# Pair products of 32 features: four stores per batch tile with batch-major rows, in place of five stores with partition-major rows

## The chip, the core and the metric

One core of a Trainium2 chip runs the whole kernel. TensorE (PE) multiplies matrices, VectorE (DVE) works elementwise, ScalarE (ACT) copies, SyncE (SP) here only issues transfers; 16 DMA engines move data between HBM and the on-chip memory SBUF, which has 128 partitions. PSUM takes the results of TensorE. The metric is device microseconds of one execution. All input and output is fp32.

## The reference

There are B = 4096 batch rows of F = 32 feature vectors of D = 64 numbers. For each of the 496 pairs of features (i, j) with i < j, vector i is multiplied by a 64x64 matrix of that pair, and the result is multiplied elementwise by vector j:

```python
i_idx, j_idx = np.triu_indices(F, k=1)
vi = inputs[:, i_idx, :]
vj = inputs[:, j_idx, :]
vdotw = jnp.einsum('bpd,pde->bpe', vi, W)
inter = vdotw * vj
return inter.reshape(B, -1)
```

A batch row gives 496 x 64 = 31,744 numbers, 126,976 bytes. The output has 520 MB, the input x 33.6 MB, the weights some 8 MB.

## The kernel before

**Tiles.** The batch is cut into NT = 32 tiles of 128 rows, one row per partition. Features are taken two at a time: pair p of the code (0 to 15) stands for features 2p and 2p+1, which give (31-2p) and (30-2p) blocks of 64 output columns, 61-4p blocks together. So pair 0 has 61 blocks and pair 15 has one. All weights stay in SBUF (w_sb, loaded once at L117); x is read tile by tile (load_x, L82 to L85), the next one at the start of each tile, on ACT's queue.

**Work in a tile.** For each pair the kernel goes over chunks of 512 columns. TensorE multiplies the transposed x by the weights of the two features into PSUM (L147), and DVE multiplies that by x and writes the product into SBUF: in one instruction for both features (L157), or in two (L166) where the second feature's chunk is shorter and the one-instruction form would write 64 columns past the end of its store's piece. That is so in the last chunk of the last pair of a store, and where the second feature has nothing left. TensorE also transposes the next tile's x at pairs 5 and 6 (L104), and ACT copies the result out of PSUM (L105).

**Stores and the ring.** DVE writes into one buffer, `ring` (L110), of RING = 28,160 elements per partition (110 KB). STORES (L18) groups the pairs; for each group the code takes the next piece of the ring, going back to 0 when the piece doesn't fit in what is left (L129 to L131), lets DVE fill it, and then SP issues one store of 128 rows for it (L172). A piece that overlaps an older store's piece can be written only when that store has landed. With blocks of 64 columns as the unit, the ring has 440 and the five groups have 118, 102, 86, 99 and 91, in sum 496. Each store is split over all 16 DMA engines, eight rows to an engine; in the trace a row is one packet, and each engine closes its share with a packet of 4 bytes.

**Where rows go.** Before the launch the host orders x as [P, NT, F*D] with the tile index moved to the front: partition p has batch rows 32p to 32p+31, one per tile. The output tensor is [P, NT * 31,744]; at L172 partition p of tile t writes to column t * cols + o0 of its own row. So rows of one store lie 32 x 126,976 = 4,063,232 bytes apart. Flattened, that is the batch order of the reference. x of one tile is one contiguous MB.

Of the kernel before, what the change touches and what calls it, by code (L numbers as in the profile page):

```python
# [1 line left out]

# [6 lines left out]

F32 = mybir.dt.float32  # L10
ALU = mybir.AluOpType

P = 128
BANK = 512
BANKS = 8
CHUNK = BANK

STORES = [[0, 1], [2, 3], [4, 5], [6, 7, 8], [9, 10, 11, 12, 13, 14, 15]]  # L18
PREFETCH_AT = [5, 6]
RING = 28160  # L20


@with_exitstack
def pair_bilinear_kernel(
    ctx: ExitStack,
    tc: tile.TileContext,
    x: bass.AP,
    w: bass.AP,
    out: bass.AP,
    F: int,  # L30
    D: int,
):

    nc = tc.nc
    NT = x.shape[0]
    NPR = F // 2

    width = [(F - 1 - i) * D for i in range(F)]
    off = [sum(width[:i]) for i in range(F)]  # L60
    cols = sum(width)
    woff = [sum(width[0 : 2 * p : 2]) for p in range(NPR)]
    store_w = [sum(width[2 * p] + width[2 * p + 1] for p in g) for g in STORES]

    const = ctx.enter_context(tc.tile_pool(name="const", bufs=1))
    xtpool = ctx.enter_context(tc.tile_pool(name="xT", bufs=2))
    psum = ctx.enter_context(tc.tile_pool(name="ps", bufs=1, space=bass.MemoryType.PSUM))

    ident = const.tile([P, P], F32, tag="ident", name="ident")
    make_identity(nc, ident)  # L70

    def runs(tl, a, b, n):

        ap = tl[:, a : a + n]
        return bass.AP(ap.tensor, ap.offset, [list(ap.ap[0]), [b - a, 2], list(ap.ap[1])])


    xbuf = [const.tile([P, (F + 1) * D], F32, tag=f"x{b}", name=f"x{b}") for b in range(2)]
    for xb in xbuf:
        nc.gpsimd.memset(xb[:, F * D :], 0.0)  # L80

    def load_x(t):  # L82
        xt = xbuf[t % 2]
        nc.scalar.dma_start(out=xt[:, : F * D], in_=x[t])
        return xt  # L85

    pring = psum.tile([P, BANKS * BANK], F32, tag="pring", name="pring")
    bank = 0

    def take_banks(n):  # L90

        nonlocal bank
        if bank + n > BANKS:
            bank = 0
        got = pring[:, bank * BANK : (bank + n) * BANK]
        bank = (bank + n) % BANKS
        return got

    def transpose_x(xT, t, xt, g):

        n = 2 * BANK // P
        pt = take_banks(2)
        for c in range(n):
            nc.tensor.transpose(pt[:, ts(c, P)], xt[:, ts(n * g + c, P)], ident)  # L104
        nc.scalar.copy(xT[:, ts(g, 2 * BANK)], pt)  # L105

    def new_xT(t):
        return xtpool.tile([P, NPR * P], F32, tag="xT", name=f"xT_{t}")

    ring = const.tile([P, RING], F32, tag="ring", name="ring")  # L110
    at = 0
    xs = {0: load_x(0)}

    w_sb = []
    for p in range(NPR):
        wp = const.tile([P, width[2 * p]], F32, tag=f"w{p}", name=f"w{p}")
        nc.sync.dma_start(out=wp, in_=w[:, woff[p] : woff[p] + width[2 * p]])  # L117
        w_sb.append(wp)

    xTs = {0: new_xT(0)}  # L120
    for g in range(2):
        transpose_x(xTs[0], 0, xs[0], g)

    for t in range(NT):
        xt, xT = xs.pop(t), xTs.pop(t)
        if t + 1 < NT:
            xs[t + 1] = load_x(t + 1)
        for s, group in enumerate(STORES):
            if at + store_w[s] > RING:  # L129
                at = 0  # L130
            osb = ring[:, at : at + store_w[s]]  # L131
            at += store_w[s]
            o0 = off[2 * group[0]]
            for p in group:
                if t + 1 < NT and p in PREFETCH_AT:
                    if t + 1 not in xTs:
                        xTs[t + 1] = new_xT(t + 1)
                    transpose_x(xTs[t + 1], t + 1, xs[t + 1], PREFETCH_AT.index(p))
                for c0 in range(0, width[2 * p], CHUNK):
                    n = [max(0, min(CHUNK, width[2 * p + h] - c0)) for h in range(2)]  # L140
                    half = -(-n[0] // BANK) * BANK
                    pm = take_banks(2 * half // BANK)
                    for b0 in range(0, n[0], BANK):
                        b1 = min(b0 + BANK, n[0])
                        for h in range(2):
                            if b0 < n[h]:
                                nc.tensor.matmul(  # L147
                                    pm[:, h * half + b0 : h * half + b1],
                                    xT[h * D : (h + 1) * D, ts(p, P)],
                                    w_sb[p][h * D : (h + 1) * D, c0 + b0 : c0 + b1],  # L150
                                    start=True,
                                    stop=True,
                                )
                    o = [off[2 * p + h] - o0 + c0 for h in range(2)]
                    xj = [(2 * p + h + 1) * D + c0 for h in range(2)]
                    if n[1] > half - BANK and o[1] + n[0] <= store_w[s]:
                        nc.vector.tensor_tensor(  # L157
                            runs(osb, o[0], o[1], n[0]),
                            runs(pm, 0, half, n[0]),
                            runs(xt, xj[0], xj[1], n[0]),  # L160
                            ALU.mult,
                        )
                    else:
                        for h in range(2):
                            if n[h]:
                                nc.vector.tensor_tensor(  # L166
                                    osb[:, o[h] : o[h] + n[h]],
                                    pm[:, h * half : h * half + n[h]],
                                    xt[:, xj[h] : xj[h] + n[h]],
                                    ALU.mult,  # L170
                                )
            nc.sync.dma_start(out=out[:, t * cols + o0 : t * cols + o0 + store_w[s]], in_=osb)  # L172


# [36 lines left out]
```

## Time and profile before

| | us |
|---|---|
| median of 4 runs | 1339.51 (1339.38 to 1339.66) |
| profiled execution, its own time | 1339.53 |
| its span on the page | 1337.8 |
| first store issued | 24.47 |
| last DVE instruction starts | 1318.2 |
| a store of 30,208-byte rows (3776 KB), issue to landing, median of 32 | 21.9 |
| x of one tile (1024 KB), issue to landing, median of 32 | 14.2 |
| DVE, 128x1024 product in one instruction, mean of 768 | 1.217 |

HBM is read for 41.94 MB and written for 520.09 MB, 420 GB/s over the span. The page's line of slices gives the mean busy share of the DMA engines as 9 tenths or more in every slice but the last of 40. How to read it: the span is what the profiler saw from the first to the last instruction; the execution's time is 1.7 us longer. A wait is put down to the releaser that came last. A DMA engine's packets in the trace overlap by a few ns, so that a busy share can go a little over 1.

### The profile page before, as it was taken

What the parts mean: (1) busy time and instruction counts of PE and PEld (TensorE: products, weight loads), DVE (VectorE), ACT (ScalarE), POOL (GpSimd) and SP (SyncE); (2) the same over time, 40 slices, a digit from 0 to 9 for tenths busy, and PEclk for the clock granted to TensorE, in tenths of its full rate; (3) what the DMA queues carried; (4) which work ended last, traced back from release to release, by engine and by line L of the source; (5) the groups of instructions that cost most, each with busy time, mean ns of one, the idle gap of its engine ahead of it and who ended that gap; (6) DMA issues with size and microseconds to landing.
All of it is one profiled execution on the core that took longest, in us unless ns stands there. A gap on an engine that the chain in (4) does not pass through costs nothing.

```text
span 1337.8 us, 13157 instructions
## 1 busy us (share of the span) xinstructions
PE 1142.3 (85%) x5376; PEld 511.6 (38%) x5376; DVE 1199.0 (90%) x1376; ACT 66.1 (5%) x65; POOL 0.9 (0%) x8
## 2 busy tenths in 40 slices
PE   7899888888988888988889989899798898888982
PEld 3344333333333443334333444334344333343431
DVE  5999889998998989989889989899898998999993
ACT  1000000000000000000000000000000000000000
POOL 0000000000000000000000000000000000000000
PEclk9999999998999989999999999999999999999997
DMA  9999999999999999999999999999999999999996
GB/s 395 427 430 433 432 427 432 425 429 432 431 428 431 423 424 431 427 424 427 418 426 417 425 435 403 429 417 427 429 419 411 430 420 432 423 413 432 422 424 272
DMA packets 30012, 562.89 MB, mean 421 GB/s; under 512 B 3456, under 2 KB 3840, under 8 KB 5376
## 3 DMA queue, kind: packets, MB, share of 16 engines
q1 hardware_dynamic: 25344, 528.49, 92.7%
q10 hardware_dynamic: 4608, 33.56, 6.0%
q8 instruction: 42, 0.69, 0.2%
q14 instruction: 18, 0.15, 0.0%
HBM read 41.94 MB, written 520.09 MB: 420 GB/s over the span
## 4 chain that ended last, share of the span: by engine, by line
DMA 43%; DVE 37%; PE 16%; issue 2%; DVEq 0%
DMA out_dram<-ring 42%; DVE ring L157 33%; PE pring L147 13%; DVE ring L166 4%; PE pring L104 3%; DMA x<-in_x_dram 1%; DVEq L157 0%; DVEq L166 0%
## 5 line engine op out<-in xcount | busy, mean ns | idle before, releaser
L157 DVE TENSOR_TENSOR ring<-pring,x 128x1024 f32<-128x1024 f32 (+3 forms) x1056 | 1114.9, 1100 | 115.7 <-DMA out_dram<-ring 53.5
L147 PE MATMUL pring<-w,xT 64*128 64x512 f32 (+4 forms) x4864 | 1074.9, 559 | 165.6 <-DVE ring L157 161.5
L147 PEld LDWEIGHTS pring<-w,xT 64*128 64x128 f32 x4864 | 451.1, 189 | 756.6 <-DVE ring L157 600.8
L105 ACT COPY xT<-pring 128x1024 f32<-128x1024 f32 x64 | 64.8, 1012 | 1193.4 <-PE pring L104 1154.9
L166 DVE TENSOR_TENSOR ring<-pring,x 128x64 f32<-128x64 f32 (+3 forms) x320 | 114.1, 381 | 3.7 <-DVE ring L157 0.5
L104 PE MATMUL pring<-ident,x 128*128 128x128 f32 x512 | 76.1, 296 | 8.3 <-DMA x<-in_x_dram 8.3
L104 PEld LDWEIGHTS pring<-ident,x 128*128 128x128 f32 x512 | 60.6, 151 | 47.8 <-issue 34.3
L105 ACT ACT_TABLE_LOAD x1 | 1.3, 1283 | 1.7 <-PEq L203 1.7
masks.py:199 POOL TENSOR_SCALAR_AFFINE_SELECT ident<-ident 128x128 f32<-128x128 f32 x1 | 0.3, 295 | 0.0
L80 POOL MEMSET x<- 128x64 f32 x2 | 0.2, 153 | 0.0
masks.py:197 POOL MEMSET ident<- 128x128 f32 x1 | 0.2, 205 | 0.3 <-POOLq L203 0.3
L203 POOL MEMSET const-bfloat16-1.0<- 128x1 bf16 x1 | 0.1, 102 | 0.0
L203 POOL MEMSET const-uint8-127<- 128x1 uint8 x1 | 0.1, 102 | 0.0
L203 POOL MEMSET const-float32-0.0<- 128x1 f32 x1 | 0.1, 99 | 0.2 <-issue 0.2
L203 POOL MEMSET const-float32-1.0<- 128x1 f32 x1 | 0.1, 99 | 0.0
## 6 DMA issues: line engine op xcount, KB each, us to landing
out_dram<-ring SPq DMA_DIRECT2D x32, 3776.0 KB, 21.9
out_dram<-ring SPq DMA_DIRECT2D x32, 3264.0 KB, 21.6
out_dram<-ring SPq DMA_DIRECT2D x32, 3168.0 KB, 22.4
out_dram<-ring SPq DMA_DIRECT2D x32, 2912.0 KB, 21.4
out_dram<-ring SPq DMA_DIRECT2D x32, 2752.0 KB, 21.5
x<-in_x_dram ACTq DMA_DIRECT2D x32, 1024.0 KB, 14.2
w<-in_w_dram SPq DMA_DIRECT2D x1, 992.0 KB, 7.3
w<-in_w_dram SPq DMA_DIRECT2D x1, 928.0 KB, 11.6
```

The source lines that it names most:

```text
L80: nc.gpsimd.memset(xb[:, F * D :], 0.0)
L104: nc.tensor.transpose(pt[:, ts(c, P)], xt[:, ts(n * g + c, P)], ident)
L105: nc.scalar.copy(xT[:, ts(g, 2 * BANK)], pt)
L147: nc.tensor.matmul(pm[:, h * half + b0 : h * half + b1], xT[h * D : (h + 1) * D, ts(p, P)], w_sb[p][h * D : (h + 1) * D, c0 + b0 : c0 + b1 ...
L157: nc.vector.tensor_tensor(runs(osb, o[0], o[1], n[0]), runs(pm, 0, half, n[0]), runs(xt, xj[0], xj[1], n[0]), ALU.mult,)
L166: nc.vector.tensor_tensor(osb[:, o[h] : o[h] + n[h]], pm[:, h * half : h * half + n[h]], xt[:, xj[h] : xj[h] + n[h]], ALU.mult,)
L203: nc = bacc.Bacc("TRN2", target_bir_lowering=False, num_devices=1)
```

## The change

The pairs are grouped into four stores in place of five. The groups have 118, 102, 123 and 153 blocks, rows of 30,208, 26,112, 31,488 and 39,168 bytes. The ring keeps its size and its rule. Batch rows are dealt out in their plain order: tile t has rows 128t to 128t+127, partition p has row 128t+p, and the output tensor is [B, 31,744]. Rows of one store then lie 126,976 bytes apart, and x needs no reordering on the host; x of one tile is still one contiguous MB. Which pair ends a group decides where L166 stands in for L157; no other instruction is touched.

```diff
-STORES = [[0, 1], [2, 3], [4, 5], [6, 7, 8], [9, 10, 11, 12, 13, 14, 15]]
+STORES = [[0, 1], [2, 3], [4, 5, 6], [7, 8, 9, 10, 11, 12, 13, 14, 15]]
...
-    NT = x.shape[0]
+    B = x.shape[0]
+    NT = B // P
...
-    cols = sum(width)
...
-        nc.scalar.dma_start(out=xt[:, : F * D], in_=x[t])
+        nc.scalar.dma_start(out=xt[:, : F * D], in_=x[ts(t, P), :])
...
-            nc.sync.dma_start(out=out[:, t * cols + o0 : t * cols + o0 + store_w[s]], in_=osb)
+            nc.sync.dma_start(out=out[ts(t, P), o0 : o0 + store_w[s]], in_=osb)
...
-    x = np.ascontiguousarray(r_inputs.reshape(P, NT, F * D).transpose(1, 0, 2))
+    x = np.ascontiguousarray(r_inputs).reshape(B, F * D)
...
-    o_d = nc.dram_tensor("out_0_dram", (P, NT * NP * D), F32, kind="ExternalOutput").ap()
+    o_d = nc.dram_tensor("out_0_dram", (B, NP * D), F32, kind="ExternalOutput").ap()
...
-    return r.results[0]["out_0_dram"].reshape(B, NP * D)
+    return r.results[0]["out_0_dram"]
```

More of the change, by code (lines that the diff above doesn't have):

```diff
@@ L181 @@
     NP = L0_rec_W.shape[0]
-    NT = B // P
-    x = np.ascontiguousarray(r_inputs.reshape(P, NT, F * D).transpose(1, 0, 2))
+    x = np.ascontiguousarray(r_inputs).reshape(B, F * D)
     wt = np.transpose(L0_rec_W, (1, 0, 2))
```

## The prediction

> **What bounds the kernel now.** The shares on the page come first: VectorE (DVE) looks fullest among the compute engines, but the 16 DMA engines are fuller.
>
> ```profile
> span 1337.8 us, 13157 instructions
> PE 1142.3 (85%) x5376; PEld 511.6 (38%) x5376; DVE 1199.0 (90%) x1376; ACT 66.1 (5%) x65; POOL 0.9 (0%) x8
> ...
> q1 hardware_dynamic: 25344, 528.49, 92.7%
> q10 hardware_dynamic: 4608, 33.56, 6.0%
> ```
>
> Stores and weight loads (q1) and x loads (q10) take 98.7% of 16 engines' span. So I ask which engine waits for which.
>
> ```profile
> DVE ring L157 <- DMA out_dram<-ring: 53.5, 35, 3.0
> DVE ring L157 <- PE pring L147: 34.2, 30, 13.2
> ```
>
> Columns: total us, times, longest. DVE stands 53.5 us waiting for old stores to leave the ring; 13.2 us of the second row is the start. Next, the busy time by stretch of the span (span, PE, PEld, DVE, ACT, POOL, clock, DMA share, GB/s).
>
> ```profile
> 51.66:90.10 38.44, 34.75 (x170) 15.46 (x168) 37.36 (x45) 2.02 (x2) 0.00 (x0) 1.00 1.00 430
> ...
> 40.00:1320.00 1280.00, 1111.91 (x5234) 496.46 (x5232) 1172.76 (x1349) 60.75 (x60) 0.00 (x0) 0.98 1.00 425
> 1325.00:1327.00 2.00, 0.00 (x0) 0.00 (x0) 0.00 (x0) 0.00 (x0) 0.00 (x0) 0.50 0.47 200
> 1327.00:1330.00 3.00, 0.00 (x0) 0.00 (x0) 0.00 (x0) 0.00 (x0) 0.00 (x0) 0.50 0.06 25
> 1330.00:1333.00 3.00, 0.00 (x0) 0.00 (x0) 0.00 (x0) 0.00 (x0) 0.00 (x0) 0.50 0.05 23
> ```
>
> The first row is a batch tile with no ring wait: compute needs 38.44 us. The second says the DMA share is 1.00 from 40 us on, although the (1337.8 - 24.5)/32 = 41.0 us available per tile exceed 38.44: the ring throttles DVE to the DMA's pace. The last two are the surprise: near the end the share is 0.06, which is 1/16. One DMA engine works alone.
>
> ```profile
> DMA packets 28, 0.26 MB, mean 22 GB/s; under 512 B 17, under 2 KB 17, under 8 KB 17
> ```
>
> This is the DMA view of 1326 to 1338 us. In the trace's packet records (one per row of a store, with its size and time) this engine ends at 1336.5 us, the other 15 at 1326.4 or so. Followed backwards from its last packet, each packet begins 3 to 4 ns before the one ahead of it ends; I find no gap down to 2 us (very early the trail may cross to another engine, since all are equally full there). **The end is therefore the sum of one engine's packets**, whatever the other 15 do.
>
> Medians over all engines are 818, 865, 940, 968 and 1119 ns for rows of 22,016, 23,296, 25,344, 26,112 and 30,208 bytes: a straight line, (1119-818)/(30208-22016) = 0.0367 ns per byte plus 9 ns. The slow engine's means are 840, 883, 957, 992 and 1155 ns, 23 ns or 2.5% above. That excess stops within some 2 us of the last DVE instruction (1318.5 us) while the other 15 still run, so it goes with computing, not with the place written to. Its cause the trace doesn't name.
>
> Its sum: 256 rows of each store group (8 per store, 32 tiles) x (840+883+957+992+1155 = 4827 ns) = 1235.7 us; 256 x rows 316 ns = 80.9; weights 21.0; 208 completion packets x 9 ns = 1.9; instruction packets 2.0; less 1,876 overlaps x 3.5 ns = 6.6. Total 1334.9; with 2 us before the first packet and 1.3 behind the last, 1338.2 against the span of 1337.8. The profiled execution took 1339.53 us, 1.7 over its span; the median of the four runs is 1339.51.
>
> **The change, part by part.**
>
> Five stores become four: per partition and tile, one packet fewer for the same 126,976 bytes. A packet's cost beyond its bytes is 9 - 3.5 = 5.5 ns net of the overlap; 256 x 5.5 = 1.4 us on the slow engine, plus 32 fewer completions x 5.5 = 0.2 us. **Gain 1.6 us**, if the 2.5% excess goes with bytes. Packets of 31,488 and 39,168 bytes aren't in the trace. They replace three packets of 840+883+957 = 2680 ns. At the slow engine's best rate (25344/957 = 26.5 B/ns) they take 2667 ns, at its worst (30208/1155 = 26.15) 2702. Net of overlaps that is -9.5 to +25.5 ns per row, so -2.4 to +6.5 us in all. I take the value by bytes, -1.4, since the excess shows no clean trend with size (36, 24, 17, 18, 22 ns from the longest to the shortest).
>
> SP issues 32 fewer stores (332 ns each) and 32 fewer waits: nothing, SP waits 1227.9 us in that place. The Trainium skill (DMA: Bandwidth & Descriptors, Anatomy of one DMA) fits a fixed cost of about 2.0 us per DMA, given for the GpSimd path; by that, 32 fewer would be worth up to 64 us. No gap between packets is open here for it to fill: a store is in flight some 22 us while the queue holds others.
>
> DVE: the last pair of a store group splits its last instruction (the L166 branch). Pairs 5 and 8 no longer end a group, pair 6 does. Per tile 480+413 ns become 819 (640 columns), 613+546 become 1080 (896), and 549 becomes two of about 347+282 (between the 64- and 256-column rows, 217 and 413). Sum -73 ns a tile, 2.3 us in all, counted at nothing: DVE's 53.5 us of ring waits swallow it.
>
> **The ring.** With 28,160 elements (440 blocks of 64) a store must lie in one piece. The new groups have 118, 102, 123 and 153 blocks: three stores per lap instead of four or five, so fewer are in flight when DVE blocks. The layout repeats every third tile. The tightest place: the 153-block store S3 begins at block 0 under S0 of the same tile (0 to 118) and waits until that has landed. Queued on the slow engine then are S1 and S2, 8 x 992 + 8 x 1204 = 17.6 us. DVE makes S3 in 38.44 x 153/496 = 11.9 us; landing to release takes 0.5 (packet end to semaphore) and issue to first packet 1.0 (first loads). **Margin 17.6 - 11.9 - 1.5 = 4.2 us**; before, by the landing times in the trace, the store ahead ends 11 to 16 us after a store's issue once the ring binds, so 10 to 15 on the same count. The first tile: S3 is issued at 51.7 us as the old last store was, and S2 keeps the engine to about 52.3 + 2.9 = 55.2: some 2.5 us left. The wait stays DVE's; behind it stand PE (PSUM full) and SP's next store. So nothing is added, but if the cover is gone, each us of lateness in S3 costs 32 us over the tiles.
>
> The other rows: x is read in contiguous blocks of 1 MB per tile before and after, equal cost. Output rows of one store lie 126,976 bytes apart instead of 4.06 MB. Packets at the present distance sit on the straight line above; weight rows, 65,536 bytes apart, do so too (7,424 bytes: 281 ns, line 282), though they are reads. The new distance lies between, nearer the weights. Bounds: today's packets run 12 us per engine above their medians in sum; no such slowing at all, or doubled, gives -12 to +12 us. I take 0. The Trainium skill (same page, Latency and other measured facts, HBM row pitch) has copies fall from 214 to 103 GB/s at 4 MiB pitch and recover with 4 KiB added. The 30,208-byte row at 1119 ns, 27 GB/s per engine, shows no such loss at 3.875 MiB; were half the rate lost today and regained, the time would halve, which the rows rule out.
>
> **Sum:** 1339.5 - 1.6 = 1337.9 us.
>
> **Rivals.**
>
> Slower, by the layout: neighbouring rows of one 16 MB band slow the writes. It hurts as soon as it reaches the slow engine, from the first percent on, at 13 us per percent; the price from the doubled excess is +12, so 1350. For it: no store of before is written that way. Against: weights and present rows both at the line. 28%.
>
> Slower, by the ring: S3 comes late. It decides when DVE and PE need over 4.2 us more for S3 than the undisturbed tile shows; the granted clock falls to 0.91 or 0.83 in stretches with waits. At 5 us, 0.8 x 32 = 26 us, 1364. Against: restarts cost DVE only 21 us on PE between 60 and 1300 us, 0.7 each. 8%.
>
> Faster, by packets: the slow engine's excess is per packet, 23 ns, and not per byte. Then 256 x 23 = 5.9 us more are saved: 1332. Against: excess is highest for the longest row. 14%.
>
> Faster, by the slow engine set free: if its excess had to do with the output rows after all, up to 5 x 23 x 256 = 29 us go, 1309. The tail speaks against it. 8%.
>
> **Numbers.** The forecast, no gap and one engine setting the end, has 42%: 1337.9, its own range 1337 to 1342. Within 0.2% (2.7 us, about what a measurement of this kernel tells from no change): 0.42. Slower 0.36 (the two rivals), faster 0.22. Range 1331 to 1352: from the per-packet case to the layout case with a little above; the freed engine and the late ring stay outside.
>
> **What would show it.** Right: q1 loses 32 x (128+16) = 4,608 packets; the window near the end still has a share of 0.06; the 30,208-byte packets stay at 1119 and 1155 ns; DVE's wait for stores rises mildly; 1,344 DVE instructions. The layout case: those two packet times rise. The ring case: DMA share under 0.98 in the middle with slices well under 420 GB/s, and DVE waiting more on PE. The freed engine: no lone engine at the end. Wrong altogether: a gap in the slow engine's packets that I took as closed.

## The result and the profile after

The changed kernel takes 1337.56 us (median of 41 runs, 1337.33 to 1337.88) against 1339.53 us (61 runs, 1339.17 to 1340.03): 1.97 us less, a ratio of 0.9985 with a 95% interval of 0.9981 to 0.9990. The small step is clear of the spread of the runs.

The page of the changed kernel, the lines that answer to those shown of before (L155 and L164 are now the two forms of the product, L145 the matmul, L102 the transpose):

```profile
span 1335.8 us, 13084 instructions
PE 1147.2 (86%) x5376; PEld 503.3 (38%) x5376; DVE 1198.8 (90%) x1344; ACT 66.1 (5%) x65; POOL 0.9 (0%) x8
...
q1 hardware_dynamic: 20736, 528.49, 92.7%
q10 hardware_dynamic: 4608, 33.56, 6.0%
```

The bytes are the same to the last digit; q1 has 25,344 - 20,736 = 4,608 packets fewer, which is 32 tiles x 128 rows plus 32 stores x 16 completions. The span is 2.0 us shorter. DVE has 32 instructions fewer and is no faster for it.

Its table of waits (total us, times, longest):

```profile
DVE ring L155 <- DMA out_dram<-ring: 68.8, 34, 3.0
PE pring L102 <- DMA x<-in_x_dram: 28.5, 22, 8.4
DVE ring L155 <- PE pring L145: 17.8, 6, 13.2
```

DVE waits 15 us longer for the ring than before. The middle row has grown; before, it held the start alone:

```profile
PE pring L104 <- DMA x<-in_x_dram: 8.3, 1, 8.3
```

Of the 28.5 us now, 8.4 are the start and 20 are 21 waits of TensorE for x. On a DMA engine a row of x takes turns with a store's row, and the rows beside it are longer now. On the slow engine (tiles 3 to 31, medians) the first packet of x follows 3.9 us after the issue in both kernels; from the first to the last of its eight packets it takes 8.2 us before, beside rows of mostly 25,344 bytes, and 11.3 us after, beside rows of mostly 39,168. The DMA issues (KB each, median us to landing):

```profile
out_dram<-ring SPq DMA_DIRECT2D x32, 4896.0 KB, 18.6
...
x<-in_x_dram ACTq DMA_DIRECT2D x32, 1024.0 KB, 17.7
```

x needs 17.7 us in place of 14.2, while the largest store lands sooner after its issue (18.6 us) than any of the five did (21.4 to 22.4): fewer stores stand ahead of it. That is the thinner cover (the cover is the work that is still queued on the DMA engines while DVE fills its next piece of the ring).

Busy time by stretch (span, PE, PEld, DVE, ACT, POOL, clock, DMA share, GB/s):

```profile
40.00:1320.00 1280.00, 1116.84 (x5234) 488.06 (x5232) 1172.23 (x1316) 60.75 (x60) 0.00 (x0) 0.99 0.99 423
1326.00:1332.00 6.00, 0.00 (x0) 0.00 (x0) 0.00 (x0) 0.00 (x0) 0.00 (x0) 0.50 0.97 418
1332.00:1334.40 2.40, 0.00 (x0) 0.00 (x0) 0.00 (x0) 0.00 (x0) 0.00 (x0) 0.50 0.08 33
```

The slow engine's stretch behind the others has shrunk. By the packet records, 14 engines finish at 1332.9 us, one at 1334.1 and the slow one at 1334.5. Before it was 14 at 1326.6 or earlier, one at 1329.6 (the prediction read all 15 as 1326.4 or so) and the slow one at 1336.5.

### The profile page after: what moved, and what is told of

Same layout as the page of the kernel before. It is cut to its first block, busy times and chain, and to the rows that moved or that the text cites. A ratio compares the mean times of both kernels' runs of the same rounds, so it can differ in the third digit from the quotient of the medians.

```text
span 1335.8 us, 13084 instructions
## 1 busy us (share of the span) xinstructions
PE 1147.2 (86%) x5376; PEld 503.3 (38%) x5376; DVE 1198.8 (90%) x1344; ACT 66.1 (5%) x65; POOL 0.9 (0%) x8
## 2 busy tenths in 40 slices
DMA packets 25403, 562.88 MB, mean 421 GB/s; under 512 B 2944, under 2 KB 3328, under 8 KB 4864
## 3 DMA queue, kind: packets, MB, share of 16 engines
q1 hardware_dynamic: 20736, 528.49, 92.7%
q10 hardware_dynamic: 4608, 33.56, 6.0%
## 5 line engine op out<-in xcount | busy, mean ns | idle before, releaser
L155 DVE TENSOR_TENSOR ring<-pring,x 128x1024 f32<-128x1024 f32 (+3 forms) x1088 | 1154.1, 1107 | 118.2 <-DMA out_dram<-ring 68.8
L145 PE MATMUL pring<-w,xT 64*128 64x512 f32 (+4 forms) x4864 | 1079.5, 556 | 141.7 <-DVE ring L155 137.3
L145 PEld LDWEIGHTS pring<-w,xT 64*128 64x128 f32 x4864 | 444.9, 187 | 749.3 <-DVE ring L155 653.4
L102 PE MATMUL pring<-ident,x 128*128 128x128 f32 x512 | 72.6, 288 | 29.1 <-DMA x<-in_x_dram 28.5
L102 PEld LDWEIGHTS pring<-ident,x 128*128 128x128 f32 x512 | 58.4, 147 | 65.3 <-issue 65.3
L164 DVE TENSOR_TENSOR ring<-pring,x 128x64 f32<-128x64 f32 (+4 forms) x256 | 71.0, 298 | 3.3
## 6 DMA issues: line engine op xcount, KB each, us to landing
out_dram<-ring SPq DMA_DIRECT2D x32, 4896.0 KB, 18.6
x<-in_x_dram ACTq DMA_DIRECT2D x32, 1024.0 KB, 17.7
```

The costliest lines, as they stand in the source:

```text
L145: nc.tensor.matmul(pm[:, h * half + b0 : h * half + b1], xT[h * D : (h + 1) * D, ts(p, P)], w_sb[p][h * D : (h + 1) * D, c0 + b0 : c0 + b1 ...
L155: nc.vector.tensor_tensor(runs(osb, o[0], o[1], n[0]), runs(pm, 0, half, n[0]), runs(xt, xj[0], xj[1], n[0]), ALU.mult,)
L164: nc.vector.tensor_tensor(osb[:, o[h] : o[h] + n[h]], pm[:, h * half : h * half + n[h]], xt[:, xj[h] : xj[h] + n[h]], ALU.mult,)
```

## Experiments

Short names: the **changed kernel** has four stores and batch-major rows; it is the base of all but the first. A time is the median of 4 to 11 runs where an interval stands beside it, else a single execution.

### The two halves of the change, each alone

Four stores with the old rows:

```diff
-STORES = [[0, 1], [2, 3], [4, 5], [6, 7, 8], [9, 10, 11, 12, 13, 14, 15]]
+STORES = [[0, 1], [2, 3], [4, 5, 6], [7, 8, 9, 10, 11, 12, 13, 14, 15]]
```

> The kernel before with the four store groups and its own row layout (rows of a store 4.06 MB apart). Theory (the slow DMA engine's packets set the end, a packet costs 5.5 ns net, the layout nothing): one packet per row and tile fewer, so the whole gain of the change, 1337.6 to 1337.9 us. Rival (the layout makes the difference, the grouping none): 1339.5.

Measured: 1337.74 us, 0.9985 (0.9976 to 0.9994) of before. The whole gain is there.

Five stores with the new rows (the same diff the other way round, in the changed kernel):

> The changed kernel with the five old store groups: the row layout alone. Theory: 1339.5, as before, within some 0.3 us. Rival (layout makes the difference): 1337.6. Rival (two effects of opposite sign that nearly cancel): neither, and run e1_four_old_layout off by as much the other way.

Measured: 1339.77 us, 1.0000 (0.9991 to 1.0009). The row layout is worth nothing here, and its profile has the long lonely tail again:

```profile
1327.00:1333.00 6.00, 0.00 (x0) 0.00 (x0) 0.00 (x0) 0.00 (x0) 0.00 (x0) 0.50 0.06 24
```

A share of 0.06 is one engine of 16. So the tail goes with the grouping, not with the layout; the two effects don't cancel, they are 2.0 and 0.

### More and fewer stores

```diff
-STORES = [[0, 1], [2, 3], [4, 5, 6], [7, 8, 9, 10, 11, 12, 13, 14, 15]]
+STORES = [[0], [1], [2], [3], [4, 5], [6, 7], [8, 9, 10], [11, 12, 13, 14, 15]]
```

> The changed kernel with eight stores per tile instead of four, rows of 11.5 to 22 KB. Theory: four packets more per row and tile, 4 x 256 x 5.5 ns = 5.6 us, and 128 completions x 5.5 ns = 0.7 us: 1337.6 + 6.3 = 1343.9. Rival (the slow engine's excess of 23 ns goes with packets, not bytes): 4 x 256 x 28.5 ns = 29.2 us and 0.7, 1367.5. The ring's cover is only greater, so DVE's waits should not rise.

Measured: 1345.31 us, 1.0041 (1.0028 to 1.0055) of before, 7.75 above the changed kernel: 1.4 us more than worked out and far from 1367.5. On the slow engine (tiles 3 to 31) the mean packets of a row add up to 4862.9 ns instead of 4822.8; less four more overlaps of 3.6 ns that is 25.7 ns, x 256 = 6.6 us, and the completions (the packets of 4 bytes) make it 7.3. A packet costs 6.4 ns there, not 5.5, and not 28.5. DVE's ring waits, which should not have risen, did:

```profile
DVE ring L155 <- DMA out_dram<-ring: 82.2, 41, 5.1
```

The DMA is 7.8 us slower over the span and DVE no slower, so DVE has more to wait (it is busy for 1192.8 us here, 1198.8 in the changed kernel); the expectation forgot that.

```diff
-STORES = [[0, 1], [2, 3], [4, 5, 6], [7, 8, 9, 10, 11, 12, 13, 14, 15]]
+STORES = [[0, 1, 2], [3, 4, 5, 6], [7, 8, 9, 10, 11, 12, 13, 14, 15]]
```

> The changed kernel with three stores per tile (171, 172 and 153 blocks), one packet fewer again. By packets alone it gains 1.6 us more: 1336.0. By the ring walk of the prediction the cover is gone: only two stores fit into a lap, so that a store is often made while only one other is in the queue (153 blocks take 12.7 us to send, 171 take 13.3 us to make), and the middle group has to wait for the store just ahead of it near its end. Gaps of about 5.7 us per two tiles, some 90 us in all: about 1430. DMA share in the middle about 0.93 instead of 0.99.

Measured: 1500.26 us, 1.1195 (1.1179 to 1.1210). Direction as the ring walk had it, the size wrong: 163 us over the changed kernel, not some 90. Its middle stretch, and its waits:

```profile
40.00:1480.00 1440.00, 1163.99 (x5232) 515.73 (x5231) 1177.32 (x1314) 60.72 (x60) 0.00 (x0) 0.93 0.88 376
```

```profile
DVE ring L155 <- DMA out_dram<-ring: 187.5, 70, 6.5
DVE ring L155 <- PE pring L145: 60.8, 68, 13.5
```

The DMA share falls from 0.99 to 0.88: the engines themselves now run dry, and all 16 end together, between 1495.2 and 1495.4 us. The walk let DVE go on at its undisturbed pace after each wait; here DVE also waits 60.8 us on TensorE in 68 pieces, with a granted clock of 0.93. That these restarts are the missing 70 us isn't shown. The gain of one more packet is buried by the cover that the third store lacks.

### What makes one engine slow

These four leave out or change computing, as each expectation says.

Stores without any computing:

```diff
+    for b in range(0, RING, 3520):
+        (nc.vector if b % 7040 else nc.gpsimd).memset(ring[:, b : b + 3520], 0.0)
...
-                                nc.tensor.matmul(
...
-                        nc.vector.tensor_tensor(
...
```

> The changed kernel without its computing: no matmul, transpose, copy or product in the loop; the ring is filled with zeros once and stored over and over, x and weights are loaded as before. Theory (the slow engine's excess goes with computing): no lone engine at the end, every packet of all engines near its median (39,168 bytes 1448 ns), about 1300 us by the sum of the medians plus some 10 us more for filling the ring: 1305 to 1315. Rival (the excess belongs to that engine or to where it writes): it stays 2.5% above, 1335 or more.

Measured: 1314.34 us. All 16 engines end between 1310.9 and 1311.4 us; there is no slow one.

Without TensorE's and ScalarE's work (matmuls, transposes and copies out, PSUM zeroed once):

> The changed kernel without TensorE's and ScalarE's work: DVE multiplies x by a PSUM that is zeroed once, so the products are zero; ring and stores as before. If the excess goes with the count of executed instructions (10,752 of 13,084 are TensorE's), 4 to 6 us of 30 stay and the time is 1306 to 1315. If it goes with DVE's work alone, the excess stays and so does 1337.

Measured: 1318.70 us. DVE does all its work here, and 15 engines end within 0.2 us of 1314.6, the last at 1315.7:

```profile
span 1316.9 us, 1776 instructions
DVE 1176.8 (89%) x1345; POOL 0.9 (0%) x8
...
q14 instruction: 13, 0.11, 0.0%
```

The queue q8 with its 42 packets of instructions, 0.69 MB, is gone from the page with TensorE's instructions. In the changed kernel none of these packets lies on the slow engine's trail behind tile 2, and nearly every row there is longer than the median, so it isn't their own time that this engine lacks. ScalarE's 64 copies are left out together with TensorE's work; no run leaves out one without the other.

Without DVE's products, TensorE at work:

> The changed kernel without DVE's products: TensorE and ScalarE work through all tiles, the ring is filled with zeros once and stored over and over. If the excess goes with TensorE's instructions, most of the 2.5% stays while TensorE runs (it may end before the stores do): 1325 to 1340. If it goes with DVE, it is gone: 1305 to 1315.

The execution took 1368.43 us, which says nothing on the stores: TensorE, with a mean clock of 0.865, ended last. The stores end between 1306.6 and 1319.3 us for 15 engines and at 1325.5 for one. A slow engine is back without DVE, 6 us behind the next.

The same count of TensorE instructions, each with a short matmul:

```diff
+    nc.vector.memset(pring, 0.0)
...
-                        b1 = min(b0 + BANK, n[0])
+                        b1 = b0 + D
```

> The changed kernel with each matmul cut to its first 64 columns: as many TensorE instructions as before, but far less time in them; the other columns of the products use what PSUM held (zeros at first), so most of the output is not the reference's. If the slow DMA engine's excess goes with the count of TensorE's instructions (or the fetching of them), it stays at some 30 us: 1337 us, the other engines done a little before it. If it goes with the time that TensorE is busy, it shrinks with it to a third or less: 1320 to 1327, against 1318.7 with no TensorE work at all.

Measured: 1481.43 us, 1.1057 (1.1038 to 1.1075): neither. The waits tell of another kernel:

```profile
DVE ring L156 <- PE pring L146: 270.5, 62, 7.9
PE pring L102 <- DMA x<-in_x_dram: 170.0, 31, 8.7
```

TensorE stands before the transposes in every tile until x has landed, the matmuls behind them wait too, and DVE runs out of PSUM. Why x, which takes 15.9 us here, comes so much later than it is wanted is left open, and the time can't decide between the two readings. The packets say more. Of the 4,096 packets of 26,112 bytes, those that took over 5 and up to 70 ns more than the median are 7.1% in the changed kernel, 6.5% here, 4.8% without DVE and 1.7% without TensorE. One engine of 16 would be 6.25%. The sum of these excesses, spread over one engine's 256 packets, is 28 ns each in the changed kernel, 27 here, 19 without DVE and 3 without TensorE. So the excess goes with TensorE's work. Whether with the count of its instructions or with the time in them isn't settled, since the short matmuls cut that time much less than the expectation took:

```profile
PE 922.6 (62%) x5376; PEld 725.0 (49%) x5376; DVE 1184.1 (80%) x1345; ACT 66.1 (4%) x65; POOL 0.9 (0%) x8
```

PE is busy for 922.6 us in place of 1147.2, 62% of the span in place of 86%. The excess hardly moved (27 against 28 ns), which speaks for the count; the 19 ns without DVE, with PE busy for 75% of the span, fit neither well. By which way TensorE's work reaches the engine (the fetching of its instructions, its semaphores), no run shows.

### Which engine it is, and sparing it

x of tiles 24 to 29 loaded in two parts by partitions:

```diff
+        cut = {24: 120, 25: 104, 26: 72, 27: 4, 28: 100, 29: 6}.get(t, P)
+        for r0, r1 in ((0, cut), (cut, P)):
```

> The changed kernel with the x loads of tiles 24 to 29 cut in two by partitions (120+8, 104+24, 72+56, 4+124, 100+28, 6+122), so that the DMA engines get different numbers of rows; the number that the slow engine gets in each tile tells which of the 16 it is. Time as the changed kernel's within 5 us. If the slow engine is the last of the 16, it gets none of tile 24's x.

Measured: 1398.76 us, 60 over what I expected. Against the changed kernel DVE begins tile 27 some 29 us late and tile 29 some 64: parts of 4, 124, 6 and 122 rows hold back x. The Trainium skill (DMA: Bandwidth & Descriptors, Why a DMA increments its semaphore by 16 and not by 1) says that such a DMA runs on the largest number of engines up to 16 that divides its rows. The trace agrees: the rule gives 114 completions for these tiles in place of 96, and the profile counts 2,962 packets under 512 bytes in place of 2,944, 18 more. By the rule, 122 rows went over two engines, 61 each. From the gaps between the slow engine's stretched packets I read 9 or 10 rows of x in tile 24, 10 in each of the next two and none in tile 27. If a DMA on k engines takes the k of lowest index, that makes it one of the engines of index 4 to 7. This reading is from a few packets and is not sure.

Then a piece of a store in four tiles, on fewer engines:

```diff
+            if s == 0 and t in (4, 11, 18, 25):
+                w0 -= 1792
+                for r0, r1 in ((0, 119), (119, 123), (123, 128)):
...
```

> The changed kernel; in tiles 4, 11, 18 and 25 the last 28 blocks (7,168 bytes a row) of the first store go out as three stores of 119, 4 and 5 rows, which should use only the lowest 7, 4 and 5 DMA engines. In the run with x loads by parts the slow engine seemed to get x rows in the patterns of engines 4 to 7. If it is the eighth (index 7) or any above the seventh, it is spared 4 x 8 x 0.27 = 8.6 us: 1337.6 - 8.6 = 1329.0, or up to some 1331 if the seven lower engines, which get 11 us more, become the last. If the slow engine is one of the lowest seven, it gets 4 x 10 x 0.28 = 11 us more: 1348.

Measured: 1361.56 us, 1.0161 (1.0147 to 1.0175). The control:

```diff
+                for r0, r1 in ((0, 120), (120, 128)):
```

> The same with the piece cut into 120 and 8 rows, which should use the lowest 15 and the lowest 8 engines: control for the extra stores. If the slow engine is index 7 it gets 9 rows in place of 8: 1337.6 + 4 x 0.3 = 1338.8. If it is the last (index 15) it is spared as much as in r1_piece_on_seven and the others hardly pay: 1329.

Measured: 1349.07 us, 1.0070 (1.0058 to 1.0083). Neither gains. By DVE's tile starts each piece costs some 5.7 us in the first and 2.8 in the second, at once and for good, and the slow engine is still the last, 2.7 us behind 14 of the others. The control should have cost 0.3 us a piece; the 2.5 us above that are a price of the extra small stores that my sum did not have. The packets show a part of it: the piece's rows of 7,168 bytes, at best 272 ns, took a mean of 414 ns in the first run and 410 in the second. The 12.5 us between the two runs are near the 11 us that an engine among the lowest seven would get. The packet records point the same way: followed back from its last packet, with gaps of up to 12 ns let through, the slow engine's trail in the first run takes in 18, 18, 18 and 19 rows of the four pieces, where it would have 8 in an uncut store and none if it were spared. So the slow one is probably among the lowest seven and was loaded rather than spared. Since the trail may change engines inside a piece, it isn't settled. No version here beats the changed kernel.

### The new wait for x

```diff
-PREFETCH_AT = [5, 6]
+PREFETCH_AT = [7, 8]
```

> The changed kernel with the next tile's transposes at pairs 7 and 8 instead of 5 and 6, which takes away the new waits of TensorE for x (22 waits, 20 us without the first). Theory: those waits lie on an engine that does not set the end: 1337.6, unchanged within 0.3 us. Rival: they cost part of what the change gained: 1336 or less.

Measured: 1338.06 us, 0.9988 (0.9979 to 0.9997) of before; the changed kernel is at 0.9985. TensorE's wait for x has left the top of the table of waits, where DVE now stands as follows, and the time has not gained:

```profile
DVE ring L155 <- DMA out_dram<-ring: 43.2, 25, 2.4
DVE ring L155 <- PE pring L145: 42.9, 38, 14.1
```

It is 0.5 us above the changed kernel, a little outside the 0.3 us of the expectation; the rival, that the waits cost a part of the gain, fails.

## Why the prediction was right

**What bounds.** The step that carried it, that the end is the sum of one engine's packets, held. Followed back in the changed kernel, the slow engine has no gap down to 2 us: 1332.6 us of packets end to end, against 1334.5 before. Taking away what slows it (TensorE's work and ScalarE's copies) brings 18.9 us in one execution, and with three stores, where the engines run dry, the sum stops setting the time.

**The size.** Forecast 1337.9, measured 1337.6; that the sum came out so near is in part luck. In the first tiles the trail of packets can be followed in more than one way, so I take tiles 3 to 31, where a tile's eight rows of x can be counted with it. There the rows' packets have means of 1152, 994, 1199 and 1478 ns, in sum 4822.8 instead of 4829.8; less one overlap of 3.6 that is 3.4 ns, x 256 = 0.9 us (said: 1.4). Completions 0.2 as said. The packets of x were 3.0 ns shorter each (313.3 in place of 316.3), some 0.8 us that no step had. The two kernels with the halves of the change give the same sums: 4822.4 ns and 313.5 for four stores, 4830.0 and 316.4 for five. Why x's packets are shorter, no run shows. The excess over the medians goes with bytes more than with packets, as taken: in sum 120 ns a row with five stores, 122 with four, 129 with eight. The eight stores put the packet at 6.4 ns rather than 5.5.

**The row layout.** Taken as nothing, between -12 and +12: nothing, by two runs. The 30,208-byte row has its median of 1119 ns in either layout.

**The ring.** The margin at the tightest store was a little optimistic: in the trace the store ahead ends 3.8 to 3.9 us after the issue in most tiles and 2.6 at the least; the sum without the 1.0 us of start gave 5.2. It sufficed. That it is a real edge, and only one store away, the three stores show.

**DVE and SP.** 73 ns a tile were counted at nothing; DVE's busy time fell by 0.2 us only, its waits rose, and neither reached the end. The sum had added the two instructions of a split in full, but they overlap: those of 480 and 413 ns take 0.81 us together.

**What was wrong.** I named a share of 0.06 near the end as a sign. One engine was alone for 6.9 us before (1329.6 to 1336.5) and is for 0.5 us now. The smaller cover that I worked out for the slow engine is also the most that the others can run ahead of it, since they stop when the ring has nothing more for them; the tail is short with four stores in both layouts and long with five in both, it is 12.8 us with eight and 0.2 with three, which fits; no run tests it alone. So 14 of them now end 1.7 us ahead instead of 10, having idled earlier, and the time doesn't care. And I counted the x loads as equal: their bytes are, but their rows now take turns with longer ones, 3.5 us later per tile, so that TensorE waits for them. That it costs nothing rests on the margin that was left, and the prediction had not counted it in.

**The rivals.** Late S3: not at four stores. Slow writes in neighbouring rows: refuted by the layout alone. Packet-bound excess: refuted by eight stores. The slow engine set free by the rows: refuted; it goes with TensorE's work.

## What to carry to other kernels

Where the DMA engines are full, look at each of them to its last packet: the mean share hid that one engine set the end and that 15 had slack. Merging stores then saves only what a packet costs beyond its bytes, here 3 to 6 ns per row, and 2 us in 520 MB with all that came with it, while it thins the cover that keeps the queue full; walk the buffer for the tightest place before merging once more, since the next step cost 12%. A transfer that shares the DMA engines with longer rows can land later, even if nothing about it was changed: x took 17.7 us here in place of 14.2.

## What was not expected of the hardware

One of the 16 DMA engines runs some 2.5% slower while TensorE executes instructions, and not while DVE alone works; the kernel without the work of TensorE and ScalarE took 18.9 us less. A second engine ends behind the other 14 too, by 3 us before and 1 after; no run looks into it. Rows of one store may lie 4.06 MB or 127 KB apart with no difference (ratio 1.0000, 0.9991 to 1.0009). A piece of 0.9 MB sent as two extra stores of 120 and 8 rows cost some 2.5 us a time beyond its bytes.
